# A four-layer graph network on one core: relu moved to ScalarE in the last batches, a third score buffer, and an instruction order planned backwards

## The chip, the cores and the metric

The kernel runs on one core of a Trainium2 chip. A core has four engines that compute: TensorE (PE in the profile; it multiplies matrices and writes its results to PSUM, which has eight banks here), VectorE (DVE), ScalarE (ACT) and GpSimd (POOL). SyncE (SP) starts the transfers. Each engine runs its own list of instructions in order, and semaphores make one wait for another. The metric is the device time of one execution in microseconds. Before the change it is 1633.63 us (median of three runs, 1631.4 to 1633.82).

## The reference, cut to what matters

The input x holds 32 batches of 512 nodes with 128 features; the adjacency matrix is 512 by 512 and shared by all batches and layers. Each layer normalizes, applies relu, runs a graph operation and adds its result to x.

```python
def _L0_gnn_ref(x, adj, W, b):            # normalized adjacency
    A_hat = adj + jnp.eye(n)
    d = jnp.sum(A_hat, axis=-1) ** (-0.5)
    A_norm = d[:, None] * A_hat * d[None, :]
    return jnp.einsum('bnc,oc->bno', jnp.einsum('nm,bmc->bnc', A_norm, x), W) + b

def step(h, _):                           # layer 1, five times
    m_in = jnp.einsum('nm,bmd->bnd', in_matrix, h)      # both matrices are adj
    ...
    z = sigmoid(av @ w3_w.T + w3_b + u3)
    r = sigmoid(av @ w4_w.T + w4_b + u3)
    hv = tanh(av @ w5_w.T + w5_b + (r * h @ u5_w.T + u5_b))
    h = (1.0 - z) * h + z * hv

# layers 2 and 3: graph attention
    h = x @ W
    e = leaky_relu(h @ a_src + (h @ a_dst) transposed, 0.2)
    attn = softmax(where(adjacent, e, -inf), axis=-1)
    out = attn @ h                        # layer 2 applies elu to it

for each layer:
    h = jnp.maximum(_layernorm(x, axis=-1), 0.0)
    x = x + layer(h)
```

## The kernel before

Everything is computed in 32-bit floats. The 32 batches run through the four layers in a staggered way: while one pair is in layer 1 (called GGNN here, five steps each), an earlier pair is in the attention layers and a later one in layer 0. The kernel doesn't issue its instructions in the order in which they are written. It records them first, each with an engine, an assumed cost and a due time, and a planner then plays the list through and picks at each moment, for each engine, the ready operation that is due first. The order in which the operations start in that play is the order in which they are issued.

```python
def run(self):
    for o in reversed(self.ops):
        o.tail = o.cost + o.delay + max((q.tail for q in o.then), default=0)
        o.first = o.waits
    uses = {v: v.uses for o in self.ops for v in o.vals}
    best = min(self.ends, key=lambda end: self.attempt(uses, *end))
    self.attempt(uses, *best)
    ...
def attempt(self, uses, last, hurry):
    ...
        o.soon = min(o.due, last - o.tail * hurry)      # what is picked first
```

Buffers are pools. A tile is taken by the operation that first needs it and given back after its last use. Those that matter here:

```python
"h_gat": tiles(3, [P, C, D + 3], "h_gat"),
"e": tiles(2, [P, C, N], "e"),            # attention scores, 128 x 4 x 512
"off": tiles(4, SMALL, "off"),
...
}, [(last, hurry) for last in (170, 173, 176, 179) for hurry in (0.06, 0.08, 0.1, 0.12)])
```

Layer 0 multiplies by the normalized matrix with Strassen-like products, seven in place of eight, which need differences of quarters of the matrix. These lie in a tile of their own, for layer 0 as for layer 1:

```python
def right_factors(mT, due):
    made = fixed([P, 4, 2, 2 * P], "made", 4)
    ...
```

The last four batches (NEAR = 4) pass through the attention in another way than the rest. The others are turned from node-major to feature-major through DRAM; the last four are turned by TensorE, and their statistics and relu are these:

```python
def center_relu(b, y, due):
    xb, st, mv, ve, rstd = xs[b], Val("st", C), Val("mv", C), Val("ve"), Val("rstd")
    for c in range(C):                                     # C = 4 chunks of 128 nodes
        op("DVE", 0.21, due, bn_stats(st[c], xb[c]))                     # L431
        op("DVE", 0.07, due, bn_aggr(mv[c], st[c]))                      # L432
        op("DVE", 0.16, due, tensor_scalar(y[c], xb[c], mean of c, 0.0,
                                           subtract, max))               # L433
    op("DVE", 0.1, due, ve = variance + EPS)                             # L436
    op("POOL", 1.0, due, rstd = ve ** -0.5)                              # L437
    return rstd
```

(The calls are shortened here; their full form is in the kernel.) Relu of the centred value is enough: the scale rstd is positive and is applied later, to the outputs of the product with the weights. The rest of the attention of one such batch, by lines of the kernel, since the profile names them:

```python
pT = to_features(y)            # L452  PE: 4 transposes into a PSUM bank
gT = copy(pT)                  # L730  ACT
q = gT @ w_aug                 # L743  PE: heads, two banks; 131 columns: h and three scores
h_gat[D:] = exp(rstd * q[D:])  # L748  ACT
off = h_gat[D] * rstd          # L751  DVE
h_gat[:D] = q[:D] * off        # L756  ACT
pr = spread of the scores      # L772  PE: 4 transposes; the tile e is taken here
e[j] = max(pr, score j) * mask # L785  DVE, four chunks j of 128 x 512
ps += e[j] @ h_gat[j]          # L794  PE: 16 matmuls of 128 x 129 in all
rden = 1 / ps[D]               # L808  DVE
layer 2: v = ps * rden; r = exp(v); v = max(v, 0) + x; x = min(r, 1) + v   # L810 DVE, L824 ACT, L825, L827 DVE
layer 3: x = ps * rden + x     # L816  DVE; then L838 stores x
```

For the earlier batches the same mixing matmuls stand in L805, the heads' scores in L759 and L761, and the store in L842. A GGNN step is L653 and L654 (reset gate), L660 (update gate), L667 and L668 (candidate) on PE, L656, L662 and L670 on ACT, L658, L672, L673 and L675 on DVE; L520 are the products with the adjacency matrix, L525 and L533 what evicts them.

Of the kernel before, what the change touches and what calls it, by code (L numbers as in the profile page):

```python
# [12 lines left out]
AF = mybir.ActivationFunctionType  # L13
ALU = mybir.AluOpType

P = 128
# [5 lines left out]
NEAR = 4  # L22
EARLY = 8
FAR0, FAR1 = 2, 4
RUN_UP = 8
LANES = 6


class Val:


    def __init__(self, kind, parts=1):
        self.kind, self.uses, self.t = kind, 0, None
        self.writers, self.readers = [[] for _ in range(parts)], [[] for _ in range(parts)]
# [5 lines left out]
class Op:  # L40
    def __init__(self, engine, cost, due, emit, delay):
        self.engine, self.cost, self.due, self.emit, self.delay = engine, cost, due, emit, delay
        self.waits, self.then, self.vals = 0, [], []


class Plan:
# [2 lines left out]

    DELAY = {"PE": 0.24, "ACT": 0.15, "DVE": 0.12, "POOL": 0.1, "SP": 2.4, "AQ": 2.4}  # L50

    def __init__(self, buffers, ends):
        self.buffers, self.ends, self.ops = buffers, ends, []

    def op(self, engine, cost, due, emit, r=(), w=(), delay=None):
        o = Op(engine, cost, due, emit, self.DELAY[engine] if delay is None else delay)
# [24 lines left out]
        o.waits = len(before)  # L81
        self.ops.append(o)

    def run(self):

        for o in reversed(self.ops):
            o.tail = o.cost + o.delay + max((q.tail for q in o.then), default=0)
            o.first = o.waits
        uses = {v: v.uses for o in self.ops for v in o.vals}
        best = min(self.ends, key=lambda end: self.attempt(uses, *end))  # L90
        self.attempt(uses, *best)
        assert self.end < math.inf, "the order has come to a stop"
        for o in self.order:
            o.emit()

    def attempt(self, uses, last, hurry):
        for v, n in uses.items():
            v.uses = n
            if v.kind:
                v.t = None  # L100
        for o in self.ops:
            o.waits = o.first

            o.soon = min(o.due, last - o.tail * hurry)
# [7 lines left out]
        now, count = 0.0, 0  # L112
# [6 lines left out]
        def start(e):  # L119
            if busy[e]:  # L120
                return
            kept = []
            while ready[e]:
                key = heapq.heappop(ready[e])
                o = self.ops[key[1]]
                opens = [v for v in o.vals if v.kind and v.t is None]
                short = [v for v in opens if len(free[v.kind]) < sum(u.kind == v.kind for u in opens)]
                if not short:
                    for v in opens:
                        v.t = free[v.kind].pop()  # L130
                    busy[e] = True
                    o.at = now
                    order.append(o)
                    post(now + o.cost, 0, o)
                    post(now + o.cost + o.delay, 1, o)
                    break
                kept.append(key)
            for key in kept:
                heapq.heappush(ready[e], key)

        def settle(o, same):
            for q in o.then:
                if (q.engine == o.engine == "PE") == same:
                    q.waits -= 1
                    if not q.waits:
                        heapq.heappush(ready[q.engine], (q.soon, q.id))

        for e in ready:
            start(e)
        while events:  # L150
            now, _, kind, o = heapq.heappop(events)
            if kind == 0:
                busy[o.engine] = False
                settle(o, True)
            else:
                done += 1
# [12 lines left out]
def gnn_stack(ctx: ExitStack, tc: tile.TileContext, a: dict, out: bass.AP):  # L169
    nc = tc.nc  # L170
    x, adj = a["x"], a["adj"]
    B, N, D = x.shape
    C = N // P
# [6 lines left out]
    def tiles(n, shape, name, pool=sb, dtype=F32):  # L180
        return [pool.tile(shape, dtype, name=f"{name}_{next(serial)}") for _ in range(n)]

    def flat(t):
        return t.rearrange("p c k -> p (c k)")

    TOKENS, SMALL = [P, C, D], [P, C]
# [19 lines left out]
        "four": tiles(2, [P, Q, W], "four"),  # L206
        "row": tiles(2, [P, N], "row"),
        "line": tiles(4, [C, Q, W], "line", dram),
        "e": tiles(2, [P, C, N], "e"),
        "v": tiles(2, TOKENS, "v"),  # L210
        "mask": tiles(2, [P, N], "mask", dtype=BF16),
        "st": tiles(4, [P, C, 6], "st"),
        "mv": tiles(4, [P, C, 2], "mv"),
        "ve": tiles(4, SMALL, "ve"),
        "rstd": tiles(8, SMALL, "rstd"),
        "off": tiles(4, SMALL, "off"),
        "rden": tiles(3, SMALL, "rden"),
    }, [(last, hurry) for last in (170, 173, 176, 179) for hurry in (0.06, 0.08, 0.1, 0.12)])
    op = plan.op
    MM, MM1, TURN = 0.858, 0.224, 0.111  # L220
    V, A = 0.61, 0.585
# [18 lines left out]
    ident = fixed([P, P], "ident")  # L240
# [14 lines left out]
    xs = []  # L255
    for b in range(B):
        v = Val("x", C)
# [31 lines left out]
    for c in range(C):  # L289
        p = Val("bank")  # L290
# [26 lines left out]
    def right_factors(mT, due):  # L317


        made = fixed([P, 4, 2, 2 * P], "made", 4)  # L320

        def quarter(a, n):
            return mT.t[:, 2 * a:2 * a + 2, n * 2 * P:(n + 1) * 2 * P]
        f = {0: (lambda: quarter(0, 0), mT), 3: (lambda: quarter(1, 0), mT), 5: (lambda: quarter(1, 1), mT)}
        f |= {k: (lambda i=i: made.t[:, i], made[i]) for i, k in enumerate((2, 1, 4, 6))}
# [100 lines left out]

    def center_relu(b, y, due):

        xb, st, mv, ve, rstd = xs[b], Val("st", C), Val("mv", C), Val("ve"), Val("rstd")
        for c in range(C):  # L430
            op("DVE", 0.21, due, lambda c=c: nc.vector.bn_stats(st.t[:, c, :], xb.t[:, c, :]), r=[xb[c]], w=[st[c]])  # L431
            op("DVE", 0.07, due, lambda c=c: nc.vector.bn_aggr(mv.t[:, c, :], st.t[:, c, :]), r=[st[c]], w=[mv[c]])  # L432
            op("DVE", 0.16, due, lambda c=c: nc.vector.tensor_scalar(  # L433
                y.t[:, c, :], xb.t[:, c, :], mv.t[:, c, 0:1], 0.0, op0=ALU.subtract, op1=ALU.max),
               r=[xb[c], mv[c]], w=[y[c]])
# [129 lines left out]
    def normalized(begun):  # L565

        anT = fixed([P, C, N], "anT", C)
        drow = Val("bank")
        dinv2 = fixed(SMALL, "dinv2")

        def turn_dinv():
            for c in range(C):
                nc.tensor.transpose(drow.t[:, c, :], dinv.t[:, c:c + 1].to_broadcast([P, P]), ident.t)
        op("PE", C * TURN, -2, turn_dinv, r=[dinv, ident, begun], w=[drow])
        op("DVE", 0.1, -790, lambda: nc.vector.tensor_mul(dinv2.t, dinv.t, dinv.t), r=[dinv], w=[dinv2])

        for m in range(C):
            op("DVE", 0.7, -1, lambda m=m: nc.vector.scalar_tensor_tensor(
                anT.t[:, m, :], adjT.t[:, m, :], dinv.t[:, m:m + 1], flat(drow.t), op0=ALU.mult, op1=ALU.mult),
               r=[adjT, dinv, drow], w=[anT[m]])  # L580
            op("DVE", 0.26, -1, lambda m=m: nc.vector.scalar_tensor_tensor(
                block(anT.t, m), ident.t, dinv2.t[:, m:m + 1], block(anT.t, m), op0=ALU.mult, op1=ALU.add),
               r=[ident, dinv2], w=[anT[m]])
        return anT, right_factors(anT, 0)


    factors = {}
# [318 lines left out]
```

## Time and profile before

| what | value |
|---|---|
| time, median of 3 | 1633.63 us |
| span of the profiled execution | 1631.2 us |
| mean granted clock of TensorE | 0.999 |
| instructions in the trace | 23929 |
| batches that go the near way (layers 2 and 3) | 28 to 31 |

A line of the view by stretches gives the stretch, its length, and then for PE, PEld (weight loads), DVE, ACT and POOL the busy time with the number of instructions in brackets; then the granted clock of TensorE (1.00 is full), the share of the DMA engines and GB/s. A 32-bit matmul appears as two records in the trace. A line of the chain that ended last gives its start, how long it held the chain, the engine, the tile written and the source line. A line of the timeline gives start, duration, engine, line, operation, tiles, shapes and, in brackets, how long the engine had stood idle before it and what ended that.

### The profile page before, as it was taken

To read this page: it belongs to the slowest core of one execution; us is meant where nothing else is said; L and a number is where in the kernel's file an instruction comes from. 1 tells how busy PE (TensorE), PEld (TensorE's weight loads), DVE (VectorE), ACT (ScalarE), POOL (GpSimd) and SP (SyncE) were. 2 spreads that over 40 slices of the span, in tenths; PEclk is the share of its full clock that TensorE was granted. 3 is DMA by queue.
4 is the path that set the end of the run, shared out by engine and by line. 5 is a ranking of instruction groups with operands and counts; after the bars stand their busy time and mean duration, and the time that the engine had idled before them with its cause. 6 is when DMAs were issued, how large, how long until landed. Compare 5 with 4: busy or idle time off the path is not lost.

```text
span 1631.2 us, 23929 instructions
## 1 busy us (share of the span) xinstructions
PE 1617.3 (99%) x7330; PEld 1169.2 (72%) x7330; DVE 1386.3 (85%) x3989; ACT 716.1 (44%) x1593; POOL 143.2 (9%) x136
## 2 busy tenths in 40 slices
PE   9999999999999999999999999999999999999998
PEld 7666666776776777777776766767677777676777
DVE  8968688898978898888898888888887888777888
ACT  5653443535335344444535345353443533434343
POOL 2200000010001100000111001110000000000001
PEclk9999999999999999999999999999999999999999
DMA  4134353534436344353433535344362323434010
GB/s 130 33 71 104 81 120 91 124 98 106 115 82 147 82 117 104 91 135 84 121 101 96 137 79 134 88 106 118 82 146 73 98 72 84 123 91 110 27 40 27
DMA packets 374176, 157.72 MB, mean 97 GB/s; under 512 B 201664, under 2 KB 355616, under 8 KB 374048
## 3 DMA queue, kind: packets, MB, share of 16 engines
q1 hardware_dynamic: 373760, 155.67, 38.5%
q8 instruction: 58, 0.95, 0.2%
q14 instruction: 70, 0.57, 0.1%
q10 hardware_dynamic: 288, 0.52, 0.1%
HBM read 86.25 MB, written 69.84 MB: 96 GB/s over the span
## 4 chain that ended last, share of the span: by engine, by line
PE 95%; DVE 3%; ACT 1%; DMA 0%; POOL 0%; issue 0%; DVEq 0%; POOLq 0%; ACTq 0%
PE bank L520 35%; PE bank L805 12%; PE bank L653 8%; PE bank L654 8%; PE bank L667 8%; PE bank L660 8%; PE bank L668 8%; PE bank L743 3%; PE bank L612 2%; PE bank L559 1%; PE bank L794 1%; DVE e L785 1%; PE bank L452 1%; POOL rstd L402 0%; DMA w<-in_L_gnn_w_w_dram 0%
## 5 line engine op out<-in xcount | busy, mean ns | idle before, releaser
L520 PE MATMUL bank<-made,S 128*128 128x256 f32 x1128 | 269.5, 380 | 1.2 <-ACT half L525 0.9
L402 POOL TENSOR_TENSOR rstd<-ve,mhalf 128x4 f32<-128x4 f32 x120 | 132.8, 1108 | 1397.5 <-DVE ve L400 1130.6
L520 PEld LDWEIGHTS bank<-made,S 128*128 128x128 f32 x1128 | 217.2, 196 | 40.4 <-issue 17.2
L525 ACT COPY half<-bank 128x256 f32<-128x256 f32 x282 | 104.4, 370 | 258.7 <-PE bank L520 255.7
L805 PEld LDWEIGHTS bank<-h_gat,e 128*128 128x128 f32 x1792 | 207.9, 192 | 13.0 <-issue 11.2
L805 PE MATMUL bank<-h_gat,e 128*128 128x129 f32 x1792 | 208.6, 275 | 0.0
L656 ACT ACTIVATE r<-bank,gate_bw 128x512 f32<-128x512 f32 x160 | 109.6, 685 | 213.5 <-PE bank L654 190.2
L672 DVE TENSOR_TENSOR hv<-hv,hT 128x512 f32<-128x512 f32 x160 | 109.3, 683 | 85.3 <-ACT hv L670 84.9
L658 DVE SCALAR_TENSOR_TENSOR rh<-r,hT 128x512 f32<-128x512 f32 x160 | 110.0, 687 | 67.4 <-ACT r L656 66.5
L653 PE MATMUL bank<-m,wT 128*128 128x512 f32 x320 | 163.7, 593 | 0.0
L667 PE MATMUL bank<-m,wT 128*128 128x512 f32 x320 | 163.4, 592 | 0.0
L654 PE MATMUL bank<-hT,wT 128*128 128x512 f32 x320 | 163.4, 592 | 0.0
L668 PE MATMUL bank<-rh,wT 128*128 128x512 f32 x320 | 163.4, 592 | 0.0
L660 PE MATMUL bank<-m,wT 128*128 128x512 f32 x320 | 163.3, 592 | 0.0
L670 ACT ACTIVATE hv<-bank,gate_bw 128x512 f32<-128x512 f32 x160 | 109.5, 684 | 118.9 <-PE bank L668 117.6
L785 DVE SCALAR_TENSOR_TENSOR e<-row,h_gat,maskT 128x512 f32<-128x512 f32 x224 | 161.4, 740 | 0.0
L520 PE MATMUL bank<-adjT,h 128*128 128x256 f32 x640 | 159.5, 380 | 0.5 <-ACT h L687 0.5
L520 PEld LDWEIGHTS bank<-adjT,h 128*128 128x128 f32 x640 | 123.3, 196 | 25.2 <-issue 13.4
L533 DVE TENSOR_TENSOR m<-half,bank 128x256 f32<-128x256 f32 x282 | 115.9, 412 | 24.3 <-ACT half L525 12.0
L662 ACT ACTIVATE z<-bank,gate_bw 128x512 f32<-128x512 f32 x160 | 109.6, 685 | 51.5 <-PE bank L660 49.8
L395 DVE BATCH_NORM_STATS2 st<-x 128x6 f32<-128x128 f32 x480 | 115.4, 279 | 4.7 <-DMA x<-in_x_dram 4.4
L654 PEld LDWEIGHTS bank<-hT,wT 128*128 128x128 f32 x320 | 60.8, 190 | 76.5 <-issue 75.1
(137 smaller groups left out, 2278.8 us busy)
## 6 DMA issues: line engine op xcount, KB each, us to landing
far<-sq SPq DMA_DIRECT2D x920, 64.0 KB
h<-far SPq DMA_DIRECT2D x240, 128.0 KB
gT<-far SPq DMA_DIRECT2D x56, 256.0 KB
row<-line SPq DMA_DIRECT2D x56, 256.0 KB
x<-in_x_dram SPq DMA_DIRECT2D x32, 256.0 KB
h<-far SPq DMA_DIRECT2D x28, 256.0 KB
out_dram<-x SPq DMA_DIRECT2D x28, 256.0 KB
hT<-far SPq DMA_DIRECT2D x104, 64.0 KB
```

Source lines behind the costliest of these rows:

```text
L395: op("DVE", 0.21, due, lambda c=c: nc.vector.bn_stats(st.t[:, c, :], xb.t[:, c, :]), r=[xb[c]], w=[st[c]])
L402: op("POOL", 1.0, due, lambda: nc.gpsimd.tensor_tensor(rstd.t, ve.t, mhalf.t, ALU.pow), r=[ve, mhalf], w=[rstd])
L520: nc.tensor.matmul(low(r), u[:, l, :], factors[k][0]()[:, l, :], start=fresh and l == 0, stop=l == 1, skip_group_check=not fresh)
L533: op("DVE", HV, due - 5, lambda: nc.vector.tensor_add(out(), u.t, low(t)), r=[u, t], w=[o])
L653: nc.tensor.matmul(flat(gate.t), gates.t[:, 0, :], flat(m.t), start=True, stop=False)
L654: nc.tensor.matmul(flat(gate.t), gates.t[:, 1, :], flat(hT.t), start=False, stop=True)
L658: op("DVE", V, due - 5, lambda: nc.vector.scalar_tensor_tensor(flat(rh.t), flat(r.t), 1.0, flat(hT.t), op0=ALU.add, op1=ALU.mult), r=[r, h ...
L660: op("PE", MM, due + 0.3, lambda: nc.tensor.matmul(flat(gate.t), gates.t[:, 2, :], flat(m.t), start=False, stop=True, skip_group_check=Tru ...
L667: nc.tensor.matmul(flat(cand.t), gates.t[:, 3, :], flat(m.t), start=True, stop=False)
L668: nc.tensor.matmul(flat(cand.t), u5T.t[:, 0, :], flat(rh.t), start=False, stop=True)
L785: op("DVE", 0.68, due + 3, lambda j=j: nc.vector.scalar_tensor_tensor(e.t[:, j, :], rows(row.t), h.t[:, j, D + 1:D + 2], mask(j), op0=ALU. ...
L805: nc.tensor.matmul(pt()[:, c, :D + 1], e.t[:, j, i * P:(i + 1) * P], h.t[:, j, :D + 1], start=(j == 0), stop=(j == C - 1))
```

## The change

It has four parts.

1. In the last four batches the relu of the centred value goes from VectorE to ScalarE. VectorE now makes the negated means (off), two chunks at a time, which ScalarE takes as its bias.
2. The differences made from layer 0's matrix are no longer in a tile of their own. They take a tile of the score pool, which has three tiles now in place of two, and give it back after the last product of layer 0. From then on the attention has three score tiles. The memory used stays the same.
3. The order is planned in rounds. After a first attempt the list is played backwards from the end (`put_off`), which gives for every operation how late it may stand. In the next attempt, operations that started after 1400 us of the plan are picked by that; those before it are picked by their due time alone. Six rounds are made from each of three settings, and the best by the plan is taken.
4. From 1420 us of the plan on, where PE would have rested 0.9 us out of the last 3.4, a transpose of the identity matrix into a free PSUM bank is put in, to keep TensorE's clock up.

```diff
+    IDLE = 0.11
+    SPAN, REST = 3.4, 0.9
...
+        for last, hurry in self.ends:
+            for again in range(6):
+                if again:
+                    late = self.put_off()
+                for o in self.ops:
+                    if not again:
+                        o.soon = min(o.due, last - o.tail * hurry)
+                    else:
+                        o.soon = late[o] / self.SLOT if o.at > self.near_end else o.due
+                self.attempt()
+                if self.end < best[0]:
+                    best = self.end, [o.soon for o in self.ops]
...
+            if e == "PE" and left and not busy[e] and now > self.idle_from and free["bank"]:
+                keep_going()
...
+            if rest < self.REST:
+                ...
+                return
+            v = Val("bank")
+            v.t, v.uses = free["bank"].pop(0), 1
+            o = Op("PE", self.IDLE, 0, lambda: self.idle(v), 0)
...
-        "e": tiles(2, [P, C, N], "e"),
+        "e": tiles(3, [P, C, N], "e"),
...
-        "off": tiles(4, SMALL, "off"),
+        "off": tiles(6, SMALL, "off"),
...
-    }, [(last, hurry) for last in (170, 173, 176, 179) for hurry in (0.06, 0.08, 0.1, 0.12)])
+    }, [(178, 0.06), (179, 0.14), (171, 0.05)], 1400,
+        IDLE_FROM, lambda v: nc.tensor.transpose(v.t[:, 0, :], ident.t, ident.t))
...
-        made = fixed([P, 4, 2, 2 * P], "made", 4)
+        made = Val("e", 4) if passing else fixed([P, C, N], "made", 4)
...
-        for c in range(C):
-            op("DVE", 0.21, due, lambda c=c: nc.vector.bn_stats(st.t[:, c, :], xb.t[:, c, :]), r=[xb[c]], w=[st[c]])
-            op("DVE", 0.07, due, lambda c=c: nc.vector.bn_aggr(mv.t[:, c, :], st.t[:, c, :]), r=[st[c]], w=[mv[c]])
-            op("DVE", 0.16, due, lambda c=c: nc.vector.tensor_scalar(
-                y.t[:, c, :], xb.t[:, c, :], mv.t[:, c, 0:1], 0.0, op0=ALU.subtract, op1=ALU.max),
-               r=[xb[c], mv[c]], w=[y[c]])
+        for a in range(2):
+            both = slice(2 * a, 2 * a + 2)
+            for c in (2 * a, 2 * a + 1):
+                op("DVE", 0.2, due, lambda c=c: nc.vector.bn_stats(st.t[:, c, :], xb.t[:, c, :]), r=[xb[c]], w=[st[c]])
+
+            def aggr(a=a, both=both):
+                for c in (2 * a, 2 * a + 1):
+                    nc.vector.bn_aggr(mv.t[:, c, :], st.t[:, c, :])
+                nc.vector.tensor_scalar_mul(off.t[:, both], mv.t[:, both, 0], -1.0)
+            op("DVE", 0.22, due, aggr, r=[st[2 * a], st[2 * a + 1]], w=[mv[a], off[a]])
+            for c in (2 * a, 2 * a + 1):
+                op("ACT", 0.385, due, lambda c=c: nc.scalar.activation(
+                    y.t[:, c, :], xb.t[:, c, :], AF.Relu, bias=off.t[:, c:c + 1]), r=[xb[c], off[a]], w=[y[c]])
...
-        return anT, right_factors(anT, 0)
+        return anT, right_factors(anT, 0, True)
```

More of the change, by code (lines that the diff above doesn't have):

```diff
@@ L24 @@
 FAR0, FAR1 = 2, 4
+IDLE_FROM = 1420
 RUN_UP = 8
@@ L42, in __init__ @@
         self.engine, self.cost, self.due, self.emit, self.delay = engine, cost, due, emit, delay
-        self.waits, self.then, self.vals = 0, [], []
+        self.id, self.waits, self.then, self.vals = None, 0, [], []
 class Plan:
     DELAY = {"PE": 0.24, "ACT": 0.15, "DVE": 0.12, "POOL": 0.1, "SP": 2.4, "AQ": 2.4}
-    def __init__(self, buffers, ends):
+    IDLE = 0.11
+    SPAN, REST = 3.4, 0.9
+    def __init__(self, buffers, ends, near_end, idle_from, idle):
         self.buffers, self.ends, self.ops = buffers, ends, []
+        self.near_end = near_end
+        self.idle_from, self.idle = idle_from, idle
     def op(self, engine, cost, due, emit, r=(), w=(), delay=None):
@@ L82, in op @@
         self.ops.append(o)
+    SLOT = 10.3
     def run(self):
+        self.before = {o: [] for o in self.ops}
         for o in reversed(self.ops):
             o.tail = o.cost + o.delay + max((q.tail for q in o.then), default=0)
[L88 to L92, printed above, removed]
+            o.first, o.after = o.waits, len(o.then)
+            for q in o.then:
+                self.before[q].append(o)
+        self.uses = {v: v.uses for o in self.ops for v in o.vals}
+        best = math.inf, None
+        for last, hurry in self.ends:
[10 more added lines that the diff above has]
+                    best = self.end, [o.soon for o in self.ops]
+                if self.end == math.inf:
+                    break
+        assert best[1], "the order has come to a stop"
+        for o, soon in zip(self.ops, best[1]):
+            o.soon = soon
+        self.attempt()
@@ L93, in run, with put_off @@
         for o in self.order:
             o.emit()
-    def attempt(self, uses, last, hurry):
-        for v, n in uses.items():
+    def put_off(self):
+        ready = {e: [] for e in self.DELAY}
+        busy = dict.fromkeys(self.DELAY, False)
+        events, late, now, count = [], {}, 0.0, 0
+        for o in self.ops:
+            o.waits = o.after
+            if not o.waits:
+                heapq.heappush(ready[o.engine], (-o.at - o.cost, o.id))
+        while True:
+            for e in ready:
+                if ready[e] and not busy[e]:
+                    o = self.ops[heapq.heappop(ready[e])[1]]
+                    busy[e] = True
+                    count += 1
+                    heapq.heappush(events, (now + o.cost, count, 0, o))
+            if not events:
+                return late
+            now, _, kind, o = heapq.heappop(events)
+            if kind == 0:
+                busy[o.engine], late[o] = False, self.end - now
+                for q in self.before[o]:
+                    count += 1
+                    heapq.heappush(events, (now + (0 if q.engine == o.engine == "PE" else q.delay), count, 1, q))
+            else:
+                o.waits -= 1
+                if not o.waits:
+                    heapq.heappush(ready[o.engine], (-o.at - o.cost, o.id))
@@ L98, in attempt @@
+    def attempt(self):
+        for v, n in self.uses.items():
             v.uses = n
@@ L102, in attempt @@
             o.waits = o.first
-            o.soon = min(o.due, last - o.tail * hurry)
         free = {k: list(reversed(v)) for k, v in self.buffers.items()}
@@ L111, in attempt @@
                 heapq.heappush(ready[o.engine], (o.soon, o.id))
-        now, count = 0.0, 0
+        now, count, work, look, left = 0.0, 0, [], 0.0, sum(o.engine == "PE" for o in self.ops)
         def post(t, kind, x):
@@ L119, in start @@
         def start(e):
+            nonlocal left
             if busy[e]:
@@ L132, in start @@
                     o.at = now
+                    if e == "PE":
+                        left -= 1
+                        work.append((now, now + o.cost))
                     order.append(o)
@@ L139, in start, with keep_going @@
                 heapq.heappush(ready[e], key)
+            if e == "PE" and left and not busy[e] and now > self.idle_from and free["bank"]:
+                keep_going()
+        def keep_going():
+            nonlocal look
+            since = now - self.SPAN
+            while work and work[0][1] <= since:
+                work.pop(0)
+            rest = self.SPAN - sum(min(b, now) - max(a, since) for a, b in work if a < now)
+            if rest < self.REST:
+                if look <= now:
+                    look = now + max(0.1, self.REST - rest)
+                    post(look, 2, None)
+                return
+            v = Val("bank")
+            v.t, v.uses = free["bank"].pop(0), 1
+            o = Op("PE", self.IDLE, 0, lambda: self.idle(v), 0)
+            o.vals.append(v)
+            busy["PE"] = True
+            order.append(o)
+            o.at = now
+            work.append((now, now + self.IDLE))
+            post(now + self.IDLE, 0, o)
+            post(now + self.IDLE, 1, o)
         def settle(o, same):
@@ L151, in attempt @@
             now, _, kind, o = heapq.heappop(events)
-            if kind == 0:
+            if kind == 2:
+                pass
+            elif kind == 0:
                 busy[o.engine] = False
@@ L155, in attempt @@
             else:
-                done += 1
+                done += o.id is not None
                 settle(o, False)
@@ L315, in gnn_stack, with right_factors @@
            r=[adjT[m], ident], w=[diag[m]])
-    def right_factors(mT, due):
-        made = fixed([P, 4, 2, 2 * P], "made", 4)
+    def right_factors(mT, due, passing=False):
+        made = Val("e", 4) if passing else fixed([P, C, N], "made", 4)
         def quarter(a, n):
@@ L324, in right_factors @@
         f = {0: (lambda: quarter(0, 0), mT), 3: (lambda: quarter(1, 0), mT), 5: (lambda: quarter(1, 1), mT)}
-        f |= {k: (lambda i=i: made.t[:, i], made[i]) for i, k in enumerate((2, 1, 4, 6))}
+        f |= {k: (lambda i=i: made.t[:, i].rearrange("p (k n) -> p k n", k=2), made[i]) for i, k in enumerate((2, 1, 4, 6))}
         for k, u, v in ((2, (0, 1), 0), (1, (1, 1), 2), (4, (1, 1), None), (6, (1, 0), 1)):
@@ L427, in center_relu @@
     def center_relu(b, y, due):
-        xb, st, mv, ve, rstd = xs[b], Val("st", C), Val("mv", C), Val("ve"), Val("rstd")
-        for c in range(C):
-            op("DVE", 0.21, due, lambda c=c: nc.vector.bn_stats(st.t[:, c, :], xb.t[:, c, :]), r=[xb[c]], w=[st[c]])
-            op("DVE", 0.07, due, lambda c=c: nc.vector.bn_aggr(mv.t[:, c, :], st.t[:, c, :]), r=[st[c]], w=[mv[c]])
-            op("DVE", 0.16, due, lambda c=c: nc.vector.tensor_scalar(
-                y.t[:, c, :], xb.t[:, c, :], mv.t[:, c, 0:1], 0.0, op0=ALU.subtract, op1=ALU.max),
-               r=[xb[c], mv[c]], w=[y[c]])
+        xb, st, mv, off, ve, rstd = xs[b], Val("st", C), Val("mv", 2), Val("off", 2), Val("ve"), Val("rstd")
+        for a in range(2):
[10 more added lines that the diff above has]
+                    y.t[:, c, :], xb.t[:, c, :], AF.Relu, bias=off.t[:, c:c + 1]), r=[xb[c], off[a]], w=[y[c]])
         op("DVE", 0.1, due, lambda: nc.vector.tensor_scalar_add(ve.t, mv.t[:, :, 1], EPS), r=[mv], w=[ve])
```

## The prediction

> **What bounds the kernel now.** I read the engine totals first, then the stretches of the last part, then the chain that ended last, then the timeline of the one stretch where the chain leaves TensorE.
>
> ```profile
> PE 1617.3 (99%) x7330; PEld 1169.2 (72%) x7330; DVE 1386.3 (85%) x3989; ACT 716.1 (44%) x1593; POOL 143.2 (9%) x136
> PEclk9999999999999999999999999999999999999999
> ```
>
> TensorE (PE) is busy 1617.3 of 1631.2 us at full clock. So 13.9 us are the most that a change of order or of the other engines can touch; only fewer matmuls could give more. The stretches (span, then busy us of PE, PEld, DVE, ACT, POOL, the clock, DMA) say where they lie:
>
> ```profile
> 50.00:200.00 150.00, 149.06 (x534) 98.97 (x533) 113.12 (x325) 68.88 (x141) 14.08 (x12) 1.00 0.32 74
> 200.00:800.00 600.00, 599.05 (x2657) 430.18 (x2656) 521.57 (x1481) 269.76 (x593) 52.80 (x48) 1.00 0.43 106
> 800.00:1400.00 600.00, 599.99 (x2695) 433.08 (x2694) 516.08 (x1441) 260.55 (x571) 47.90 (x44) 1.00 0.41 102
> ...
> 1600.00:1610.00 10.00, 9.57 (x82) 8.94 (x81) 10.00 (x35) 3.92 (x12) 1.53 (x2) 1.00 0.01 2
> 1610.00:1620.00 10.00, 7.96 (x56) 7.49 (x55) 8.74 (x36) 4.09 (x17) 1.01 (x1) 0.83 0.09 26
> 1620.00:1631.20 11.20, 6.77 (x61) 6.58 (x59) 6.40 (x21) 0.69 (x3) 0.00 (x0) 1.00 0.25 72
> ```
>
> From 200 to 1400 us PE rests 0.96 us in all. The start (0 to 50) holds 2.7, 50 to 200 holds 0.9, and the stretches of 20 us from 1460 to 1600 hold 0.74, 0.46, 0.48, 0.13, 0.00, 0.03 and 0.57. Then come 0.43, 2.04 and 4.43; of the last, 4.40 lie after PE's last matmul (1626.8 to 1631.2): normalize, store, done. VectorE (DVE) is full in 1600 to 1610, ScalarE (ACT) 39%. The chain confirms it. From 1439.9 it is mostly PE, with short excursions at 1465 and 1523, but from 1585.2 to 1614.4 it is DVE nearly alone:
>
> ```profile
> 1587.20 1.55 DVE st L431 x8
> 1588.75 0.54 DVE mv L432 x8
> 1589.29 1.55 DVE y L433 x8
> ...
> 1607.25 0.57 DVE y L433 x3
> ...
> 1613.00 1.33 DVE e L785 x2
> ...
> 1614.38 1.12 PE bank L772 x4
> 1615.49 2.80 PE bank L794 x16
> ```
>
> In that stretch of 29.2 us DVE is busy 29.14, PE 26.16, ACT 13.28. So after the last GGNN step (batches 30 and 31) the kernel is bound by DVE, and PE pays twice. It waits, and it then runs slowly, as the timeline of PE shows:
>
> ```profile
> 1613.57 0.69 PE L452 MATMUL bank<-ident,y 128*128 128x128 f32 x4 [1.93 <-ACT h_gat L756]
> 1614.38 1.12 PE L772 MATMUL bank<-ident,h_gat 128*128 128x128 f32 x4
> 1615.28 3.01 PE L794 MATMUL bank<-h_gat,e 128*128 128x129 f32 x16
> ```
>
> The wait ends with ACT's L756, which scales the heads out of their PSUM bank; the transpose L452 takes a bank, most likely that one. In the timeline L756 itself waited 0.80 us for DVE's small product off L751, which stood in line behind stats and relus. So here too DVE is the one that is late.
>
> **What the Trainium skill says.** "TensorE: Matmul & The Clock Gate", Part 1, says that the clock falls to half after an idle window of about 3.4 us. The trace agrees in size: a clock of 0.83 over 10 us is 3.4 us at half speed, a loss of 1.7 us (12.4 us at 0.88, from 1614.4, gives 1.5). "ScalarE: Activation LUTs", Rules for kernel authors, says to use VectorE for relu. That is a rule for one instruction; here DVE is full and ACT half idle. Its section What ACT_TABLE_LOAD costs gives 280 ns + 0.833 ns an element with a bias pointer, so an estimate of 387 ns at 128, and an overlap of 93 ns back to back. The nearest in the trace (L756, 128x128, one pointer) takes 387 ns, and six in a row 1.66 us, so 0.26 each when packed. "Perfetto Trace Analysis", Identifying the Most-Contended Engine, warns that matmul busy time isn't distance from the best; so below I count PE work by its step, not by its busy sum.
>
> **Part 1, relu to ACT.** It is in batches 28 to 31 (NEAR = 4), 2 layers of 4 chunks: 32 DVE instructions y leave, 16 small ones (off, the negated means) come, and 32 ACT ones. By the timeline y steps at 0.19 us (4 end to end in 0.85, one is 0.27), off at about 0.08. DVE: -32 x 0.19 + 16 x 0.08 = -4.8 us. ACT: +32 x 0.26 to 0.39 = +8 to +12 us, over some 90 us in which it is under half busy. The latency of one layer of one batch grows by about 0.7 us: four relus take 1.2 to 1.5 on ACT against 0.76 on DVE, and there is one more handover.
>
> **Part 2, the third score buffer.** The differences made from layer 0's matrix live in a tile of the pool e, which is given back after the last layer-0 product (about 1440 us). PE then has three score tiles for the attention of the last batches: PE can still be reading two while DVE fills the third. It takes no work away. The transpose L772, which needs a free e, waits in the trace but little (0.4 us of weight load), so alone I give it under 1 us.
>
> **Part 3, the order.** I compared the instruction order of the two built programs. PE has 3745 instructions in both, of the same kinds, so PE's work is unchanged. POOL's order is the same; PE's first differs at instruction 257, long before the tail. What counts is how much attention is left after the last candidate matmul (L668). On PE: 128 mixing matmuls L794/L805 before, 156 after (+28 x 0.223 = +6.2), 24 and 28 heads (+0.9), one gate step of 2 x 0.86 no longer behind it (-1.7). So 41.8 us of PE work stand there before and 47.3 after (0.223: 8 records, two an instruction, in 0.89 us). On DVE after the last hT: -20 y (-3.8), +10 off (+0.8), +4 e (+4 x 0.66 = 2.6), +10 finishing steps (+10 x 0.26), +5 reciprocals (0.4), a scaling and its transpose (1.0), one x less (-0.6): from 39.6 to 42.6 us. So the order keeps back PE work, 5.5 us of it, to be done beside a DVE stage that grows by 3.0 only. Before, DVE set the pace with 39.6 against 41.8; afterwards PE has 4.7 us more than DVE rather than 2.2.
>
> **Part 4, the identity transposes.** The built program has none: no matmul in it reads ident alone. The planner found no window with 0.9 us of rest. This part costs and gives nothing; the clock is kept only if PE indeed rests less.
>
> **The sum.** Before, the last candidate ends at 1578.16 and PE at 1626.77: 48.6 us for 41.8 of work, so 6.8 lost (rests, slow clock, restarts). Earlier rests from 1445 to 1578.2: 1.8. Nothing at the start, in the middle or in the last 4.4 us can go. If PE is fed throughout, 8.6 us are won. If DVE stays the pace: the last candidate comes 5.5 earlier, plus about half of the 1.8, and DVE's stage is 3.0 longer: 5.5 + 0.9 - 3.0 = 3.4 us won. I take a point between, nearer the second, because DVE and PE are close to even and each wait for a chain of DVE, ACT and PE still costs: 5 us. The time was 1633.6 (2.4 above the profile's span), so 1628.6 us.
>
> **The rivals.** (a) DVE still bounds the tail: 42.6 us of DVE work stand there, each layer's statistics wait for the layer before it, and the clock dips again. Then 3.4 us or less are won: 1630 to 1632. For it: DVE at 100% now. Against it: the count above. (b) The relu's way over ACT becomes a wait: 8 layers of batches at 0.7 us laid bare, 5.6 us, would eat the gain: about 1633. Against it: ACT at 13.28 of 29.2 and several batches in flight. (c) The new order opens holes in the middle, where it had 0.96 us in 1200: 2 to 6 us of waits on far transfers would give 1631 to 1636. Against it: DVE has 14% slack there and the work is the same. (d) PE is fed throughout: 1625.
>
> **Range and chances.** The range goes from (d) to a mild (c): 1625.5 to 1633. Two per cent are 33 us, more than twice all of PE's rest, so faster by that is out of reach; slower by it would need holes of 33 us. Hence 0.01, 0.98, 0.01.
>
> **What would show it.** Right: PE's rest from 1460 to its last matmul falls from 4.9 to under 2.5 us; the clock there is 0.95 or more; the chain's DVE stretch of 29 us breaks into PE pieces; 32 relus on ACT at 0.3 to 0.4 us; 200 to 1400 still under 2 us of rest; the end after the last matmul still about 4.4. Wrong: DVE at 100% over 20 us or more with PE resting beside it, PE waiting for ACT's y, or rests in the middle.

## The result and the profile after

The changed kernel takes 1623.93 us (median of six runs, 1623.67 to 1625.04) against 1633.57 (six of the kernel before): a ratio of 0.9945, interval 0.9932 to 0.9957, so about 9 us less. The prediction said 1628.6 (1625.5 to 1633.0): the direction was right, the size was half of what came, and the time lies below the range.

The totals of the page after:

```profile
PE 1612.4 (99%) x7330; PEld 1167.8 (72%) x7330; DVE 1379.9 (85%) x3973; ACT 724.5 (45%) x1625; POOL 146.2 (9%) x136
...
PEclk9999999999999999999999999999999999999999
```

PE's busy time fell by 4.9 us though its instructions are the same, 7330 records; the rest of the 9.1 us of span is less rest. The stretches after, with the columns of before:

```profile
50.00:200.00 150.00, 149.07 (x545) 101.42 (x544) 113.00 (x320) 68.59 (x143) 12.73 (x11) 1.00 0.31 72
200.00:800.00 600.00, 599.66 (x2654) 429.05 (x2653) 520.79 (x1481) 266.03 (x587) 55.51 (x48) 1.00 0.44 107
800.00:1400.00 600.00, 600.00 (x2701) 433.79 (x2700) 514.81 (x1450) 262.30 (x577) 49.22 (x45) 1.00 0.42 104
...
1600.00:1610.00 10.00, 9.24 (x81) 8.79 (x80) 9.82 (x39) 6.79 (x25) 2.01 (x2) 1.00 0.10 27
```

Start and middle are as before. The last part is better seen cut at its own events: the end of the last candidate matmul (L668, now L764), the last matmul, the end. The cut of before lies at the end of that matmul's record; its counterpart after is 1568.90, and the cut there lies 0.16 us ahead of it, where the next matmul starts. First before, then after:

```profile
1440.00:1578.16 138.16, 136.32 (x648) 97.58 (x647) 114.78 (x319) 56.51 (x132) 9.76 (x9) 1.00 0.28 73
1578.16:1626.80 48.64, 45.57 (x364) 42.53 (x363) 43.60 (x158) 18.66 (x64) 5.00 (x5) 0.96 0.06 17
1626.80:1631.20 4.40, 0.00 (x0) 0.00 (x0) 1.54 (x8) 0.00 (x0) 0.00 (x0) 0.99 0.42 119
```

```profile
1440.00:1568.74 128.74, 128.53 (x626) 93.70 (x625) 106.59 (x299) 59.31 (x141) 9.93 (x9) 1.00 0.28 71
1568.74:1617.80 49.06, 48.12 (x425) 47.29 (x423) 46.46 (x167) 23.91 (x83) 5.21 (x5) 1.00 0.11 33
1617.80:1622.10 4.30, 0.00 (x0) 0.00 (x0) 1.53 (x8) 0.00 (x0) 0.00 (x0) 0.75 0.43 122
```

The stage behind the last candidate is as long as before (49 us), but PE handles 425 records in it instead of 364, at full clock. The end comes 9.0 us earlier because the last candidate comes 9.25 us earlier (1568.90 for 1578.16). The way out after the last matmul is unchanged. DVE is busy 46.5 of the 49 us.

The chain that ended last (start, length, what):

```profile
1566.37 0.70 ACT hv L766
...
1567.09 0.69 DVE hv L768
1567.78 0.66 DVE e L881
...
1587.09 3.73 DVE e L881 x6
...
1600.47 0.66 DVE v L906 x2
...
1606.88 0.61 PE bank L868 x4
1607.49 1.79 PE bank L890 x16
```

From 1567 to 1606.9 it is DVE nearly throughout, for 40 us where it was 29. The chain names DVE although PE rests next to nothing: two engines are full at once, and the chain has to choose one.

**Where the 9 us lay.** A way to count PE's lost time without its busy sum: give every matmul its step in an uninterrupted run (two records each: 0.858 us at 512 columns, 0.433 at 256, 0.223 at 129 or 131; 0.111 for a transpose), add up along the instruction order, 1606 us in both kernels, and subtract from the time at which the step of the last one ends on the trace. (Steps taken to another digit shift both columns by some 2 us, but not the differences between them.)

| lost by PE, in all, up to | before | after |
|---|---|---|
| the last layer-0 group (L612, L708; from 1332.6 and 1331.4 us) | 9.75 | 9.44 |
| the last candidate's step (1577.99 and 1568.74) | 13.78 | 9.94 |
| the last mixing matmul's step (1626.60 and 1617.59) | 20.56 | 11.55 |

So 3.5 us were won between 1332 and the last candidate, 5.2 behind it, 0.3 earlier. About 1.9 of the 9 go with the clock: of the 123 executions of before that were timed beside the experiments, 58 have a mean clock of 1.000 and a median of 1631.4 us, and 65 have 0.999 or 0.998, as the trace of before does, and 1633.2.

### The profile page after: what moved, and what is told of

Read it like the earlier page. It is cut to its first block, busy times and chain, and to the rows that moved or that the text cites. A ratio compares the mean times of both kernels' runs of the same rounds, so it can differ in the third digit from the quotient of the medians.

```text
span 1622.1 us, 24005 instructions
## 1 busy us (share of the span) xinstructions
PE 1612.4 (99%) x7330; PEld 1167.8 (72%) x7330; DVE 1379.9 (85%) x3973; ACT 724.5 (45%) x1625; POOL 146.2 (9%) x136
## 4 chain that ended last, share of the span: by engine, by line
PE 94%; DVE 4%; POOL 0%; DMA 0%; issue 0%; ACT 0%; SPq 0%; DVEq 0%; POOLq 0%; ACTq 0%
PE bank L616 34%; PE bank L901 11%; PE bank L749 8%; PE bank L750 8%; PE bank L764 8%; PE bank L763 8%; PE bank L756 8%; PE bank L839 3%; PE bank L708 2%; DVE e L881 1%; PE bank L890 1%; PE bank L655 1%; PE bank L548 0%; DVE x L912 0%; DMA e<-in_adj_dram 0%; DVE st L522 0%
## 5 line engine op out<-in xcount | busy, mean ns | idle before, releaser
L616 PE MATMUL bank<-made,S 128*128 128x256 f32 x960 | 230.6, 380 | 0.3 <-DVE m L629 0.3
L901 PE MATMUL bank<-h_gat,e 128*128 128x129 f32 x1792 | 211.9, 275 | 0.0
L616 PEld LDWEIGHTS bank<-made,S 128*128 128x128 f32 x960 | 184.2, 196 | 29.9 <-issue 11.4
L766 ACT ACTIVATE hv<-bank,gate_bw 128x512 f32<-128x512 f32 x160 | 109.7, 686 | 120.8 <-PE bank L764 120.5
L764 PE MATMUL bank<-rh,wT 128*128 128x512 f32 x320 | 163.4, 592 | 0.0
L764 PEld LDWEIGHTS bank<-rh,wT 128*128 128x128 f32 x320 | 60.8, 190 | 76.5 <-issue 67.4
```

The costliest lines, as they stand in the source:

```text
L616: nc.tensor.matmul(low(r), u[:, l, :], factors[k][0]()[:, l, :], start=fresh and l == 0, stop=l == 1, skip_group_check=not fresh)
L764: nc.tensor.matmul(flat(cand.t), u5T.t[:, 0, :], flat(rh.t), start=False, stop=True)
L901: nc.tensor.matmul(pt()[:, c, :D + 1], e.t[:, j, i * P:(i + 1) * P], h.t[:, j, :D + 1], start=(j == 0), stop=(j == C - 1))
```

## The experiments

"Before" below is always the kernel before, run beside; a difference is the ratio times 1633 us.

**One part at a time.** First the relu alone (the old planner):

```diff
+ op("ACT", 0.385, due, activation(y[c], xb[c], Relu, bias=off[c]))     # part 1, and off made on DVE
- op("DVE", 0.16, due, tensor_scalar(y[c], xb[c], mean, 0.0, subtract, max))
```

> The kernel before with part 1 alone: relu of batches 28 to 31 on ScalarE, the old planner, two score tiles. Theory 'VectorE relief' (the 29 us stage in which VectorE was full set the end, so 4.8 us less work there is most of the gain): 3 to 5 us faster than before. Theory 'order' (the gain comes from what the backward plan puts beside what; relief alone is not used): within 2 us of before. The kernel's own plan ends 2.6 us later than before's, so by it: about 2.6 us slower.

Measured: 1636.04 us, ratio 1.0020 (1.0013 to 1.0028): 3.3 us slower. VectorE has less to do and the kernel is later. The waits of PE from 1440 on (engine, tile, line, whom it waited for: us in all, times, longest) show why. First before, then with the relu alone:

```profile
PE bank L452 <- ACT h_gat L756: 1.9, 1, 1.9
PE bank L794 <- DVE e L785: 1.0, 2, 0.6
PE bank L520 <- ACT half L525: 0.9, 2, 0.5
PE bank L520 <- ACT h L687: 0.5, 1, 0.5
PE bank L520 <- DVE m L533: 0.3, 1, 0.3
```

```profile
PE bank L801 <- DVE e L792: 2.3, 2, 1.4
PE bank L527 <- DVE S L515: 2.0, 2, 1.8
PE bank L527 <- ACT half L532: 1.4, 3, 0.5
PE bank L779 <- ACT h_gat L763: 0.8, 1, 0.8
PE bank L459 <- DVE off L758: 0.7, 1, 0.7
...
```

These waits lie in GGNN products (L527) as well as in the attention: another order came out of the old planner, and it is a worse one. Relief alone, with this planner, is not the cause; what the relu would do in before's own order was not run. 'Order' expected within 2 us and missed by 1.3.

The third tile alone:

```diff
-        made = fixed([P, 4, 2, 2 * P], "made", 4)
+        made = Val("e", 4) if passing else fixed([P, C, N], "made", 4)
-        "e": tiles(2, [P, C, N], "e"),
+        "e": tiles(3, [P, C, N], "e"),
```

> The kernel before with part 2 alone: the third score tile from layer 0's factors, the old planner, relu on VectorE. Theory 'buffer' (PE's mixing waits for score tiles): 2 us or more faster. Theory 'order': within 2 us. The kernel's own plan ends 1.6 us later than before's.

Measured: 1634.64, ratio 1.0014 (1.0007 to 1.0021), 2.3 us slower, 0.3 outside what 'order' allowed. Both together, with the old planner:

> Parts 1 and 2 without the new planner. If relief and buffer make the gain together: 6 us or more faster than before. Theory 'order': within 3 us of before, on either side. The kernel's own plan ends 3.3 us later than before's.

Measured: 1637.55, ratio 1.0029 (1.0018 to 1.0040), 4.7 us slower, where 'order' allowed 3. So neither resource brings anything to the old planner. The new planner alone (relu on VectorE, two score tiles):

```diff
-        best = min(self.ends, key=lambda end: self.attempt(uses, *end))
+        for last, hurry in self.ends:
+            for again in range(6): ...            # part 3, as in the change
```

> Part 3 (and 4) alone: rounds of backward planning, relu on VectorE, two score tiles. Here the plan does put in 18 identity transposes. Theory 'order': 4 to 6 us faster, about half of the gain of all parts, since VectorE still has its 4.8 us of relu. Theories 'relief' and 'buffer': under 2 us. The kernel's own plan ends 3.5 us earlier than before's.

Measured: 1628.83, ratio 0.9977 (0.9967 to 0.9987), 3.8 us faster: less than half of the 9.

**The changed kernel less one part.** Without the third tile:

```diff
-        "e": tiles(3, [P, C, N], "e"),             # and made is a tile of its own again
+        "e": tiles(2, [P, C, N], "e"),
```

> Parts 1, 3 and 4 without the third score tile: the changed kernel with two score tiles. If the order has to have relief on VectorE to win: 7 us or more faster than before. If it has to have the third tile: about the 4 us of the order alone. The kernel's own plan ends 4.4 us earlier than before's.

Measured: 1628.58, ratio 0.9976 (0.9966 to 0.9986), 3.9 us faster: the relu adds nothing to the order alone. Without the relu:

```diff
+ op("DVE", 0.16, due, tensor_scalar(y[c], xb[c], mean, 0.0, subtract, max))   # relu back on VectorE
```

> Parts 2, 3 and 4, relu on VectorE: the changed kernel without part 1. If the third tile is what the order needs: 6 to 8 us faster than before. If VectorE's relief is: about 4 us. The kernel's own plan ends 6.9 us earlier than before's.

Measured: 1624.77, ratio 0.9951 (0.9934 to 0.9968), 8.0 us faster. Order and third tile together make nearly all of the gain; the relu's part in it, about 1 us, is within the intervals. The planner's own end, known before a run, had put the ends of these six at +2.6, +1.6, +3.3, -3.5, -4.4 and -6.9 us against that of before; measured are +3.3, +2.3, +4.7, -3.8, -3.9 and -8.0. PE's waits from 1440 on in the changed kernel, in the one without the third tile, and in the one without the relu:

```profile
PE bank L839 <- ACT gT L826: 0.7, 1, 0.7
PE bank L548 <- DVE v L906: 0.2, 1, 0.2
```

```profile
PE bank L889 <- DVE e L880: 0.9, 3, 0.5
PE bank L838 <- ACT gT L825: 0.6, 1, 0.6
PE bank L547 <- DVE rden L903: 0.5, 1, 0.5
PE bank L306 <- DVE v L905: 0.3, 1, 0.3
```

```profile
PE bank L883 <- DVE e L874: 1.7, 1, 1.7
```

With two tiles PE waits for scores three times, and once, at L306, it is an idle transpose that waits. From 1570 to 1620 DVE is busy 43.6 us there and 46.7 in the changed kernel: with a tile less it stands idle 3 us more.

**How the third tile acts.** Either it takes waits away when the kernel runs, or it lets the planner choose another order. So the kernel without the third tile got one in its finished order:

```diff
+        # the order is planned with two score tiles; layer 0's factors hold a third till about 1440 us
+        for v in sorted(first, key=first.get):       # then tiles are given out along that order
+            for u in [u for u in held if last[u] < first[v]]:
+                held.remove(u); free.append(u.t)     # the third one joins in when it is free
+            v.t = spare if v.kind == "f" else free.pop(0)
```

> The kernel with relu and order but two score tiles (parts 1, 3, 4), in exactly its own instruction order, with the third score tile handed round when the instructions are issued, after the order is fixed. If the third tile helps by taking waits for a free tile away at run time: as fast as the changed kernel, 1624. If it helps only through the other order that the planner can make with it: within 0.7 us of the two-tile kernel, 1628.6.

Measured: 1627.83, ratio 0.9975 (0.9964 to 0.9985), the 0.9976 of the two-tile kernel again. The tile is worth 4 to 5 us, and within the intervals (1.6 us either way) all of it comes through the order that can be planned with it.

**The identity transposes.** The order alone does put in 18; here its plan and banks are kept and they are not issued:

```diff
-        IDLE_FROM, lambda v: nc.tensor.transpose(v.t[:, 0, :], ident.t, ident.t))
+        IDLE_FROM, lambda v: None)
```

> The order-only kernel with the same plan and the same banks, but the 18 identity transposes not issued. If they keep the clock: slower by 1 to 2 us than with them, and a granted clock clearly under 1 in some stretch after 1560 us. If they change nothing: within 0.5 us of it.

Measured: 1628.41, ratio 0.9974 (0.9965 to 0.9984) against 0.9977 with them: no difference, and the clock is 1.00 throughout to 1620 us without them (the longest rest there is 0.84 us). Part 4 brings nothing, in the changed kernel because none is issued and here because the clock stays up anyway. Where a rest is long enough to lower the clock, it wasn't tried.

**Was VectorE the pace?** In the next runs work is taken from VectorE or added to it. First, with the order kept, the kernel before, with statistics over 8 of 128 features in batches 28 to 31 (work left out):

```diff
-  bn_stats(st.t[:, c, :], xb.t[:, c, :])
+  bn_stats(st.t[:, c, :], xb.t[:, c, :8])
```

> The kernel before in its own instruction order, with the statistics of batches 28 to 31 taken over 8 of the 128 features (work left out: the output is not the reference's). VectorE does about 0.1 us less in each of 32 instructions, so 3 to 4 us less, 2 to 2.5 of it in the stage after the last GGNN step. Theory 'VectorE was the pace of that stage': 1.5 to 3 us faster. Theory 'the order of waits sets it, not VectorE's work': under 0.7 us.

Measured: 1630.34, ratio 0.9986 (0.9980 to 0.9993), 2.3 us faster, for 2.8 us less of DVE busy time (1386.3 to 1383.5). Part of it goes with the clock: PE's longest rest behind the candidate fell from 1.93 to 1.43 us, and 19 of the 20 executions have a mean clock of 1.000, of before 16 of 33. Among those alone the medians differ by 1.0 us. So in the order of before VectorE did hold up the end, but not one to one, and in part through the clock. The same on the changed kernel:

> The counterpart of the thinned statistics of before, on the changed kernel in its own order: statistics of batches 28 to 31 over 8 of the 128 features (work left out). 3 to 4 us less on VectorE. If PE is fed: 0 to 0.7 us faster than the changed kernel, as PE loses only 1.8 us there. If VectorE is still the pace: 2 us or more.

Measured: 1623.41, ratio 0.9944 (0.9930 to 0.9958), where the changed kernel has 0.9945: nothing, for 3.3 us less of VectorE. There PE is the limit: from the last candidate to its last matmul it loses 1.6 us in all. The other direction, every statistics instruction given twice, on the changed kernel:

```diff
-  lambda c=c: nc.vector.bn_stats(st.t[:, c, :], xb.t[:, c, :])
+  lambda c=c: [nc.vector.bn_stats(st.t[:, c, :], xb.t[:, c, :]) for _ in range(2)]
```

> The changed kernel in its own instruction order, each of the 32 statistics instructions of batches 28 to 31 given twice (the same result written twice): 0.19 us x 32 = 6.1 us more work on VectorE, about 3.9 of it after the last GGNN step. Theory 'PE is fed, VectorE has slack again': under 1.5 us slower than the changed kernel. Theory 'VectorE and PE are even, nearly all of VectorE's work shows': 3 to 4 us slower.

Measured: 1635.71, ratio 1.0019 (1.0012 to 1.0026): 12 us slower than the changed kernel, against both expectations. The groups by form (busy us, mean ns, idle before) of the changed kernel and of this one:

```profile
L522 DVE BATCH_NORM_STATS2 st<-x 128x6 f32<-128x128 f32 x32 | 7.6, 281 | 0.0
```

```profile
L522 DVE BATCH_NORM_STATS2 st<-x 128x6 f32<-128x128 f32 x64 | 17.0, 287 | 1.1
```

The load itself was mis-sized: the second writing to the same place does not overlap the first, so DVE is busy 9.0 us more (1388.9 against 1379.9), not 6.1. Even so each us cost 1.3. A part of that is one wait at 1530 us; in the stretches, from 1526 us:

```profile
1526.00:1530.00 4.00, 3.57 (x22) 3.18 (x21) 3.79 (x20) 1.86 (x6) 0.90 (x1) 1.00 0.00 0
1530.00:1533.00 3.00, 0.87 (x7) 0.47 (x6) 2.79 (x15) 1.46 (x5) 0.44 (x2) 1.00 0.00 0
1533.00:1537.00 4.00, 4.00 (x11) 2.25 (x9) 2.65 (x5) 0.76 (x2) 1.11 (x1) 0.58 0.00 0
```

PE rests 2.1 us and then runs 4 us at a clock of 0.58, a loss of 1.7 more. The same load on before's order:

> The kernel before in its own order with the same 32 instructions given twice. If VectorE is simply the pace after the last GGNN step (20 of the 32 are there): about 4 us slower than before. If any added work on VectorE is multiplied by waits, as in the changed kernel: 8 us or more.

Measured: 1644.05, ratio 1.0071 (1.0055 to 1.0088): 12 us slower than before, for 8.9 us more of DVE: the second expectation held. The clock falls twice in this trace, at 1597.6 and 1624.9, and once in that of before. So the changed order is no more brittle than the old one. And with the planner told of the load (0.4 us in place of 0.2):

```diff
-  op("DVE", 0.2, due, lambda c=c: nc.vector.bn_stats(...))
+  op("DVE", 0.4, due, lambda c=c: [nc.vector.bn_stats(...) for _ in range(2)])
```

> The changed kernel with every one of the 32 statistics instructions given twice, as in the run that was 11.8 us slower than it, but the planner is told their true cost and makes its order anew. If the 6 us of VectorE work themselves were what cost: 6 us or more over the changed kernel. If the order, tight around wrong costs, was: 3 to 6 us over it (the plan ends 4.5 us later).

Measured: 1632.21, ratio 0.9999 (0.9990 to 1.0007), 8.8 us over the changed kernel by the ratios, 8.3 by the times. Planning anew saves 3 us of the 12; the rest is the work itself (8.6 us of DVE busy time more than the changed kernel), one to one. VectorE has no slack for more in any of these three orders, though in the changed one there is nothing to win from less.

**Has ScalarE room?** Every relu given twice on the changed kernel, order kept:

```diff
+  for _ in range(2): nc.scalar.activation(y[c], xb[c], Relu, bias=off[c])
```

> The changed kernel in its own order, each of the 32 relus on ScalarE given twice (the same result): about 0.26 to 0.3 us x 32 = 8 to 10 us more on ScalarE, and some 0.6 us more from the statistics to the transposes of each of the 8. Rival 'the way over ScalarE becomes a wait': 3 us or more slower. 'ScalarE has room': under 1.5 us.

Measured: 1628.83, ratio 0.9976 (0.9967 to 0.9985), 5.1 us slower. ACT has 12.4 us more of relu (64 at 397 ns for 32 at 396) in a stage in which it was half idle. PE rests for it: in its waits from 1440 on, 0.7 us for the heads' scores, 0.7 for gT, 0.6 and 0.5 for ACT's copies of products and 0.4 for y. ScalarE is not full, but what it does is on the way.

**More rounds.** Nine rounds from the first setting:

```diff
-            for again in range(6):
+            for again in range(9):                  # and only the setting (178, 0.06)
```

> The changed kernel with nine rounds of the backward plan from the first of the three settings, in place of six from each. Its plan ends 0.4 us earlier than the changed kernel's, with a different order in the last part. If the plan's end decides: 0 to 1 us faster than the changed kernel. If the order of two plans that end alike differs on the chip by chance: within 1 us on either side.

Measured: 1623.82, ratio 0.9947 (0.9933 to 0.9960): the changed kernel's time.

## Why the prediction was wrong

**Right.** What can be won lies in PE's lost time; PE's work is unchanged; start, middle (0.34 us of rest from 200 to 1400) and the way out (4.3 us) don't change; no identity transpose is issued; PE's rest from 1460 to its last matmul fell to 1.1 us and the clock there is 1.00; 32 relus came to ACT at 396 ns. Rivals (b) and (c), a bare way over ScalarE and holes in the middle, did not come.

**The step that failed: the sum for a DVE that stays the pace.** "If DVE stays the pace: the last candidate comes 5.5 earlier, plus about half of the 1.8, and DVE's stage is 3.0 longer". The 5.5 was right (5.4 us of PE work more stand behind the candidate). DVE did stay full, and its stage is 2.5 us longer (from the end of the last hT, the new state of the last GGNN step, to its own last instruction: 43.4 us before, 45.9 after). But the last candidate came 9.25 earlier, not 6.4, and the last hT followed it after 4.5 us in place of 6.8 (1573.4 against 1584.9). 9.25 + 2.3 - 2.5 = 9.0. Two terms failed:

- "Earlier rests from 1445 to 1578.2: 1.8", of which half was taken, so 0.9. It was PE's recorded rest, while the lost time from 1332 to the candidate was 4.0 us and 3.5 of it was won (and 0.3 ahead of 1332). A matmul's record runs 0.16 us into the next one (275 ns long at a step of 111, 592 at 429), so each restart costs 0.16 us more than the rest that is shown, and a shorter hold-up shows none. For the stage behind the candidate I had counted by steps (6.8), for the stretch ahead of it I had not.
- The gate step "no longer behind it (-1.7)" was booked as PE work alone. In before, the update gate's matmuls (L660) follow the last candidate; ScalarE waits for them, does z first and starts the candidate's tanh (L670) 3.1 us after the candidate. Now they come first, and the tanh (L766) starts 0.04 us after it. Before, then after:

```profile
1577.14 1.02 PE L668 MATMUL bank<-rh,wT 128*128 128x512 f32 x2
1577.99 1.88 PE L660 MATMUL bank<-m,wT 128*128 128x512 f32 x4
1579.05 0.69 ACT L662 ACTIVATE z<-bank,gate_bw 128x512 f32<-128x512 f32 x1 [3.60 <-PE bank L660]
...
1581.24 0.72 ACT L670 ACTIVATE hv<-bank,gate_bw 128x512 f32<-128x512 f32 x1
```

```profile
1566.17 1.02 PE L756 MATMUL bank<-m,wT 128*128 128x512 f32 x2
...
1567.88 1.02 PE L764 MATMUL bank<-rh,wT 128*128 128x512 f32 x2
...
1568.94 0.69 ACT L766 ACTIVATE hv<-bank,gate_bw 128x512 f32<-128x512 f32 x1 [1.03 <-PE bank L764]
```

DVE gave back 0.8 of these 3.1 us by other work in between, and hT is ready 2.3 us sooner after the candidate. No run moves this step alone; that it makes the 2.3 us is read from the traces.

Rival (d), "PE is fed throughout: 1625", was therefore the nearest, and too slow as well, since its 8.6 us had the same 1.8 in it. "A point between, nearer the second" chose the wrong side: with 3.3 us less work on DVE the changed kernel is no faster, so DVE was no longer the pace alone. (The range was said to begin at (d), but 1633.6 - 8.6 is 1625.0, not 1625.5.)

**Wrong about the parts.** "It takes no work away ... so alone I give it under 1 us": alone, the third tile costs 2.3 us, and with the order it is worth 4 to 5. I had looked for waits that it would end; it has none to end, and it works through what the planner can place. The relu's 4.8 us on DVE were counted in full and bring about 1 us, not separable from none. And one sign was false: "the chain's DVE stretch of 29 us breaks into PE pieces". It grew to 40. A long DVE stretch says that DVE is full, not that PE waits.

**Open.** What exactly the planner does with the third tile isn't settled. With two tiles VectorE idles 3 us more from 1570 to 1620, which fits, but no run isolates it.

## What to carry to other kernels

Where a planner sets the order, a part is not worth its own saving: the third tile made the old planner's result 2.3 us slower and the new one's 4 to 5 us faster, so play the planner through for each combination and compare on the chip. Count what the binding engine has lost by its step in uninterrupted runs, not by its recorded rest, over the whole stretch and not only where the rest is seen. When two engines are full at once, the chain names one of them; taking work away (nothing, for 3.3 us) and adding it (8.8 to 12 us, for 9) tell what it means.

## What the runs showed of the hardware

The Trainium skill ("TensorE: Matmul & The Clock Gate", Part 1) speaks of an idle window of about 3.4 us before the clock falls. Here it fell with no rest that long. In before, the longest rest ahead of the fall was 1.93 us and PE was busy 1.48 of the 3.41 us from 1610.65; then it had half the clock for 3.41 us. In the doubly loaded kernel it was busy 1.29 of 3.42 us, and then had half the clock for 3.41. The length of a rest alone does not decide. Relu alone, and relu and tile with the old planner, have the same rest of 1.77 us up to 1494.6 and almost the same busy time of PE around it; the clock fell in the second and stayed at 1.00 in the first. The same two stretches, relu and tile first:

```profile
1492.82:1496.23 3.41, 1.39 (x5) 0.98 (x6) 3.38 (x9) 0.00 (x0) 0.00 (x0) 1.00 0.44 115
1496.23:1499.64 3.41, 2.95 (x7) 1.88 (x7) 0.06 (x1) 0.37 (x1) 0.00 (x0) 0.50 0.82 229
```

```profile
1492.82:1496.23 3.41, 1.40 (x5) 1.00 (x6) 3.38 (x9) 0.00 (x0) 0.00 (x0) 1.00 0.40 115
1496.23:1499.64 3.41, 2.49 (x10) 1.59 (x10) 0.57 (x3) 0.74 (x2) 0.00 (x0) 1.00 0.66 212
```

So one trace with a full clock does not show that a rest is harmless; 1.70 us (order and tile without the relu) left it at 1.00 too.

Of two BATCH_NORM_STATS2 that write the same place, the second starts 0.31 us after the first, in the doubly loaded kernel; those to different places step at 0.19 to 0.20 in the changed kernel.
